# Post-norm stack with sparse experts: the loads of the experts' results issued in both arms of the branch, three unused products instead of five

## The chip, the cores and the metric

The kernel runs on one core of one Trainium2 chip. The metric is the device time of one execution in microseconds (us). The kernel before took 748.87 us, the median of three runs from 746.87 to 749.79.

## The reference

Two layers work on 2048 tokens of width 128. The change lies behind the last of their parts, a mixture of experts:

```python
probs = softmax(flat @ router_w)
topw, topi = top_k(probs, 2)                       # two of E = 8 experts for each token
combine = sum(one_hot(topi, E) * topw[..., None], axis=1)
h = silu(einsum('td,edf->tef', flat, w1) + b1)     # F = 512
y = einsum('tef,efd->ted', h, w2) + b2
out = einsum('te,ted->td', combine, y)
x = layernorm(x + (res + out))                     # then the last norm, and the output
```

Each token's output is the normed sum of a part that the kernel has in SBUF (`x4s`) and of the weighted results of the token's two experts.

## The kernel before

The tokens are 16 tiles of 128 in four blocks of four (`NB` = 4, `TB` = 4). Each token's row is first scattered to a DRAM table `xr`, sorted by expert, by indirect DMAs of GpSimd's queue. The experts then work on blocks of 256 rows (`BK`), each for one expert: `fetch_rows` (line 1379) loads a block from `xr` through SP's queue, `copy_weights` picks the expert's weights on VectorE, `first` and `second` (lines 1413 and 1426) are the two products with the activation between them, and `back` turns the result (line 1439), weighs it (line 1442) and scatters it by two indirect DMAs (line 1444) to a DRAM table `yr` of 4096 rows: row t holds token t's first expert's result, row 2048 + t its second's.

Since every expert's last block may be partly empty, up to 23 blocks (`NBK`) can be needed, and the number needed, `many`, is known at run time only. The first 19 blocks (`OFTEN`) always run. The last four stand under a branch, line 1490, which every engine takes for itself. The arm that is run when there are no more than 19 blocks holds no line of the source. The build puts steps into it that raise the completion counters (semaphores) by what the other arm would have raised, so that the counters agree behind the branch whichever arm ran. SP and ACT's transfers share eight such counters and take them in turn; GpSimd's indirect DMAs have another eight.

Behind the branch comes the last part. For each of the four blocks b, two loads of 256 KB bring the results of the first and second experts from `yr` into SBUF tiles `yk`, one issued by SP and one by ACT (line 1507): eight loads in all, called first to eighth here in the order b = 0 (SP, ACT), b = 1 (SP, ACT) and so on. A product with the identity puts `x4s` into a PSUM tile `z5` for each block (line 1499, from line 1510), then five products that nobody reads follow (`warm`, line 1513), and then, block after block, two more products with the identity add the block's two `yk` tiles (`sum_up`, line 1499 from line 1519). An fp32 product is two passes of TensorE. Of each block, VectorE then takes the statistics (lines 1043, 1044 and 1524), GpSimd the root (line 1066), VectorE the shift (line 1531), and ACT, with VectorE's help in the last block, writes the normed rows (lines 1048 and 1538), which SP stores (line 1541). This order is held on each engine as written.

Of the kernel before, what the change touches and what calls it, by code (L numbers as in the profile page):

```python
# [9 lines left out]
F32 = mybir.dt.float32  # L10
# [8 lines left out]
P = 128  # L19
# [8 lines left out]
def tile_postln_stack(ctx: ExitStack, tc: tile.TileContext, a: dict, out: bass.AP):  # L28
    nc = tc.nc
    T, D = a["x"].shape  # L30
    NT = T // P
    TB = 4
    BW = TB * P
    NB = NT // TB
# [9 lines left out]
    NBK = 2 * T // BK + E - 1  # L44
# [81 lines left out]
    def bc(v):  # L126
        return v.unsqueeze(1).to_broadcast([P, TB, D])
# [25 lines left out]
    with ExitStack() as l0:  # L153
# [419 lines left out]
        for k in range(NQ):  # L573
            b = k // 2
# [449 lines left out]
    for e in range(0, E, 2):  # L1024
        nc.sync.dma_start(
            out=wall[:, e : e + 2],
            in_=a["we"].rearrange("(e p) c -> p e c", p=P)[:, e : e + 2],
# [10 lines left out]
    lm = ctx.enter_context(tc.tile_pool(name="l1m", bufs=3))  # L1038
# [273 lines left out]
    for step in SEQUENCE.split():  # L1312
        name, of = step.split(":")
# [45 lines left out]
    def registers(n, engine, top):  # L1359
# [10 lines left out]
    many = nc.values_load(  # L1370
        used[0:1, :],
        min_val=0,
        max_val=NBK,
        skip_runtime_bounds_check_because="so many blocks at most",
    )

    def fetch_rows(j):
        xb = lm.tile([P, KT, ROW], F32, name="xb", bufs=SOON + 2)
        nc.sync.dma_start(
            out=xb, in_=xr[bass.ds(firsts[j], BK), :].rearrange("(t p) c -> p t c", p=P)  # L1380
        )
        xbs[j] = xb
# [3 lines left out]
    def copy_weights(j):  # L1386
        wt = lm.tile([P, WC], F32, name="wt", bufs=AHEAD)
        nc.vector.tensor_copy(wt, flat[:, bass.ds(offsets[j], WC)])
        wts[j] = wt

    def turn_rows(j):
        xb = xbs[j]
        pt = ps.tile([P, KT, P], F32, tag="p", name="px5")
        for t in range(KT):
            nc.tensor.transpose(pt[:, t, :], xb[:, t, 0:D], ident)  # L1395
        xT = lm.tile([P, BK], F32, name="xT5")
        nc.vector.tensor_scalar(
            xT,
            pt.rearrange("p t d -> p (t d)"),
            cols[:, 2:3],  # L1400
            cols[:, 3:4],
            ALU.mult,
            ALU.add,
        )
        xTs1[j] = xT

    def first(j):
        wt, xT = wts[j], xTs1.pop(j)
        hu = lm.tile([P, NF, BK], F32, name="hu", bufs=2)
        for f in range(0, NF, 2):  # L1410
            pu = ps_a.tile([P, 2, BK], F32, tag="acc", name="pu")
            for n in range(2):
                nc.tensor.matmul(pu[:, n], wt[:, ts(f + n, P)], xT, start=True, stop=True)  # L1413
                nc.scalar.activation(  # L1414
                    hu[:, f + n],
                    pu[:, n],
                    AF.Silu,
                    bias=wt[:, 2 * NF * P + f + n : 2 * NF * P + f + n + 1],
                )
        hus[j] = hu  # L1420

    def second(j):
        wt, hu = wts.pop(j), hus.pop(j)
        acc = ps_a.tile([P, BK], F32, tag="acc", name="acc")
        for f in range(NF):
            nc.tensor.matmul(  # L1426
                acc, wt[:, ts(NF + f, P)], hu[:, f], start=(f == 0), stop=(f == NF - 1)
            )
        yT = lm.tile([P, KT, P], F32, name="yT5")
        nc.vector.tensor_scalar(  # L1430
            yT.rearrange("p t d -> p (t d)"), acc, wt[:, WC - 1 : WC], None, ALU.add
        )
        yTs[j] = yT

    def back(j):
        xb, yT = xbs.pop(j), yTs.pop(j)
        pt = ps.tile([P, KT, P], F32, tag="p", name="py5")
        for t in range(KT):
            nc.tensor.transpose(pt[:, t, :], yT[:, t, :], ident)  # L1439
        yb = lm.tile([P, KT, D], F32, name="yb")  # L1440
        for t in range(KT):
            nc.vector.tensor_scalar_mul(yb[:, t], pt[:, t], xb[:, t, D + 1 : D + 2])  # L1442
        for t in range(KT):
            put = nc.gpsimd.indirect_dma_start(  # L1444
                out=yr[:, :],
                out_offset=bass.IndirectOffsetOnAxis(
                    ap=xb.bitcast(U32)[:, t, D : D + 1], axis=0
                ),
                in_=yb[:, t, :],
                in_offset=None,  # L1450
                bounds_check=2 * T - 1,
                oob_is_err=False,
            )
            tc.declare_no_dep(put.ins, group="back", reason="every row is written once")
            tc.add_to_no_dep_group("back", put.ins)
        return put

    def experts(begin, end):

        put = None  # L1460
        for j in range(begin, min(begin + AHEAD - 1, end)):
            copy_weights(j)
        for j in range(begin, min(begin + SOON, end)):
            fetch_rows(j)
        turn_rows(begin)
        for j in range(begin, end):
            if j + SOON < end:
                fetch_rows(j + SOON)
            first(j)
            if j + 1 < end:  # L1470
                turn_rows(j + 1)
            if j > begin:
                put = back(j - 1)
            second(j)
            if j + AHEAD - 1 < end:
                copy_weights(j + AHEAD - 1)
            if 4 <= j < 4 + NB:
                bt = ts(j - 4, TB)
                with tc.issue_after(put.ins):
                    nc.gpsimd.tensor_tensor(x3s[:, bt, :], x3s[:, bt, :], bc(mixc), ALU.subtract)  # L1480
            if 4 + NB <= j < 4 + 2 * NB:
                bt = ts(j - 4 - NB, TB)
                with tc.issue_after(put.ins):
                    nc.gpsimd.tensor_tensor(x4s[:, bt, :], x3s[:, bt, :], x4s[:, bt, :], ALU.add)
        back(end - 1)


    OFTEN = NBK - E // 2
    experts(0, OFTEN)
    with tc.If(many > OFTEN, preferred_fallthrough_block=False):  # L1490
        experts(OFTEN, NBK)

    y_v = yr.rearrange("(k n p) d -> k p n d", k=2, p=P)


    yks, zs, mvs, rs, nbs = {}, {}, {}, {}, {}

    def add(b, src, start, stop):
        nc.tensor.matmul(  # L1499
            zs[b], ident, src.rearrange("p t d -> p (t d)"), start=start, stop=stop  # L1500
        )

    for b in range(NB):
        bt = ts(b, TB)
        yk = [lm.tile([P, TB, D], F32, tag="mid", name=f"yk{k}", bufs=8) for k in range(2)]
        for k in range(2):
            (nc.sync, nc.scalar)[k].dma_start(out=yk[k], in_=y_v[k, :, bt, :])
        yks[b] = yk
        zs[b] = ps.tile([P, BW], F32, tag="p", name="z5")
        add(b, x4s[:, bt, :], True, False)  # L1510
    warm = ps_a.tile([P, BW], F32, tag="acc", name="warm2")
    for _ in range(5):
        nc.tensor.matmul(
            warm, ident, x4s[:, NT - TB :].rearrange("p t d -> p (t d)"), start=True, stop=True
        )
# [100 lines left out]
```

## Time and profile before

| | |
|---|---|
| median of three runs | 748.87 us |
| the profiled execution: its time | 749.07 us |
| its span, first to last instruction | 747.4 us |
| mean granted TensorE clock | 0.961 |
| PE, DVE, ACT, POOL busy | 89%, 72%, 63%, 26% |
| indirect DMAs of line 1444 | 38, two for each of 19 blocks: the arm with the last four blocks did not run |
| last of these begins on POOL | 721.61 us |
| loads of line 1507 begin | 725.84 us |
| first add of a `yk` begins on PE | 729.85 us |
| last work of VectorE on the output | 742.50 us |

Times in the trace are in microseconds from the span's start. PE is TensorE, PEld its weight loads, DVE is VectorE, POOL is GpSimd; a q behind an engine's name means its instruction queue, where branches, counter steps and DMA issues stand. Between the profiled execution's span and its time lie 1.67 us.

### The profile page before, as it was taken

To read this page: it belongs to the slowest core of one execution; us is meant where nothing else is said; L and a number is where in the kernel's file an instruction comes from. 1 tells how busy PE (TensorE), PEld (TensorE's weight loads), DVE (VectorE), ACT (ScalarE), POOL (GpSimd) and SP (SyncE) were. 2 spreads that over 40 slices of the span, in tenths; PEclk is the share of its full clock that TensorE was granted. 3 is DMA by queue.
4 is the path that set the end of the run, shared out by engine and by line. 5 is a ranking of instruction groups with operands and counts; after the bars stand their busy time and mean duration, and the time that the engine had idled before them with its cause. 6 is when DMAs were issued, how large, how long until landed. Compare 5 with 4: busy or idle time off the path is not lost. (4 is left out here: it accounts for less than half of the span.)

```text
span 747.4 us, 10679 instructions
## 1 busy us (share of the span) xinstructions
PE 662.8 (89%) x3745; PEld 376.5 (50%) x3745; DVE 535.4 (72%) x893; ACT 469.4 (63%) x1080; POOL 196.8 (26%) x203
## 2 busy tenths in 40 slices
PE   8989999999889988998799988799999805999984
PEld 7766655444346543533343333246567502688851
DVE  2566798897689887987899879796895634365524
ACT  1768798877787886877697778644455522344412
POOL 2311210112020130200500004014342676268632
PEclk9989999999999999999999999899999956999998
DMA  5902240210000205200069930150500011312115
GB/s 132 269 3 58 57 100 16 58 40 17 1 1 1 57 4 113 57 0 1 0 128 204 192 57 1 40 103 13 215 1 4 29 40 39 80 58 63 36 36 154
DMA packets 43622, 46.29 MB, mean 62 GB/s; under 512 B 3164, under 2 KB 33378, under 8 KB 43568
## 3 DMA queue, kind: packets, MB, share of 16 engines
q1 hardware_dynamic: 38896, 39.79, 23.8%
q0 software_dynamic: 2272, 4.24, 1.6%
q10 hardware_dynamic: 2400, 1.57, 0.8%
q8 instruction: 30, 0.49, 0.3%
q14 instruction: 24, 0.20, 0.1%
HBM read 23.13 MB, written 14.45 MB: 50 GB/s over the span
## 5 line engine op out<-in xcount | busy, mean ns | idle before, releaser
L637 ACT ACTIVATE sc<-sc,nmx 128x1024 f32<-128x1024 f32 (+7 forms) x384 | 321.6, 838 | 98.7 <-DVE nmx L634 65.4
L619 PE MATMUL sc<-kT,q 64*128 64x512 f32 (+7 forms) x1536 | 297.1, 509 | 19.0 <-ACT sc L637 17.9
L634 DVE TENSOR_REDUCE nmx<-sc 128x1 f32<-128x1024 f32 (+3 forms) x256 | 273.6, 1116 | 33.3 <-PE sc L619 19.8
L619 PEld LDWEIGHTS sc<-kT,q 64*128 64x128 f32 x1536 | 122.1, 187 | 143.1 <-ACT sc L637 86.7
L342 POOL TENSOR_TENSOR prod<-q,kT 128x1024 f32<-128x1024 f32 x16 | 37.4, 2348 | 203.5 <-PE pdl L354 68.9
L637 ACT ACTIVATION_READ_ACCUMULATOR sc<-sc,nmx 128x1 f32 x384 | 75.8, 197 | 0.0
L1414 ACT ACTIVATE hu<-pu,wt 128x256 f32<-128x256 f32 x76 | 33.4, 474 | 59.6 <-PE pu L1413 56.6
L627 DVE TENSOR_REDUCE nmx<-sc 128x2 f32<-128x256 f32 (+3 forms) x64 | 51.6, 818 | 11.7 <-PE sc L611 11.1
L94 POOL TENSOR_TENSOR ln_rs<-ln_rs,half_m 128x4 f32<-128x4 f32 x8 | 8.3, 1038 | 182.6 <-DVE ln_rs L93 182.6
L611 PE MATMUL sc<-rmask,lmask 64*128 64x64 bf16 x512 | 50.7, 190 | 0.0
L1444 POOL DMA_INDIRECT yr<-yb,xb x38 | 41.2, 1085 | 35.3 <-DVE yb L1442 28.4
L1413 PE MATMUL pu<-xT,wt 128*128 128x256 f32 x152 | 41.1, 393 | 0.1
L611 PEld LDWEIGHTS <-lmask 64*128 64x128 bf16 x512 | 28.0, 102 | 20.6 <-issue 13.4
L1276 POOL DMA_INDIRECT xr<-rows,slots x32 | 32.0, 999 | 19.9 <-issue 15.1
L1426 PE MATMUL acc<-hu,wt 128*128 128x256 f32 x152 | 35.9, 379 | 0.0
L317 PE MATMUL pq<-x2T,pq 128*128 128x256 f32 x128 | 33.5, 407 | 1.2 <-DMA pq<-in_pq_dram 0.6
L445 PE MATMUL pv<-x2T,pv 128*128 128x512 f32 x64 | 32.2, 633 | 2.6 <-DVE wx L451 2.2
L457 PE MATMUL py<-wx,po 128*128 128x512 f32 x64 | 30.8, 612 | 0.0
L1413 PEld LDWEIGHTS pu<-xT,wt 128*128 128x128 f32 x152 | 26.7, 189 | 7.6 <-ACT hu L1414 3.5
L317 PEld LDWEIGHTS pq<-x2T,pq 128*128 128x128 f32 x128 | 24.2, 198 | 11.0 <-ACT sc L637 6.3
L1426 PEld LDWEIGHTS acc<-hu,wt 128*128 128x128 f32 x152 | 27.5, 190 | 3.2
L1430 DVE TENSOR_SCALAR yT<-acc,wt 128x256 f32<-128x256 f32 x19 | 9.2, 484 | 23.4 <-PE acc L1426 23.3
(268 smaller groups left out, 798.5 us busy)
## 6 DMA issues: line engine op xcount, KB each, us to landing
xr<-pad SPq DMA_DIRECT2D x10, 845.0 KB
q<-q SPq DMA_DIRECT2D x32, 256.0 KB
wx<-wd SPq DMA_DIRECT2D x8, 1024.0 KB
wall<-in_we_dram SPq DMA_DIRECT2D x4, 1029.0 KB
xb<-xr SPq DMA_DIRECT2D x19, 130.0 KB
x2T<-in_xT_dram SPq DMA_DIRECT2D x4, 256.0 KB
xs<-in_x_dram SPq DMA_DIRECT2D x4, 256.0 KB
yk<-yr SPq DMA_DIRECT2D x4, 256.0 KB
```

The lines of the kernel that those rows point to most:

```text
L317: nc.tensor.matmul(pm[:, n // 2, ts(n % 2, QW)], pq[:, ts(c + n, P)], x2T[:, ts(k, QW)], start=True, stop=True,)
L342: nc.gpsimd.tensor_tensor(prod, q.rearrange("p c (t e r) -> p c t e r", e=2, r=HT)[:, :, :, eo], kT[:, :, eo, ts(k, QT), :], ALU.mult,)
L445: nc.tensor.matmul(pm[:, j], pv[:, ts(c + j, P)], x2T[:, ts(b, BW)], start=True, stop=True)
L611: nc.tensor.matmul(o[:, w - HT :], lmask[r, eo], rmask[r], start=False, stop=True,)
L619: nc.tensor.matmul(o, qs[k][eo][r, c, ts(t, P)], kT[r, c, eo, n0 : n0 + nt, :], start=True, stop=(g < NG - 1),)
L627: nc.vector.tensor_reduce(nm, sc.rearrange("p e (j x) -> p j e x", j=2)[:, :, :, :w], AX.XY, ALU.min,)
L634: nc.vector.tensor_reduce(nm, sc[:, :, :w], AX.XY, ALU.min)
L637: nc.scalar.activation(o, o, AF.Exp, bias=nm[:, n : n + 1], scale=-1.0, accum_out=sm[:, i % TB, 2 * c + j, g : g + 1],)
L1413: nc.tensor.matmul(pu[:, n], wt[:, ts(f + n, P)], xT, start=True, stop=True)
L1414: nc.scalar.activation(hu[:, f + n], pu[:, n], AF.Silu, bias=wt[:, 2 * NF * P + f + n : 2 * NF * P + f + n + 1],)
L1426: nc.tensor.matmul(acc, wt[:, ts(NF + f, P)], hu[:, f], start=(f == 0), stop=(f == NF - 1))
L1444: put = nc.gpsimd.indirect_dma_start(out=yr[:, :], out_offset=bass.IndirectOffsetOnAxis(ap=xb.bitcast(U32)[:, t, D : D + 1], axis=0), in_= ...
```

## The change

The eight `yk` tiles are allocated ahead of the branch. A function `load_results` issues the eight loads, in the same order and from the same two queues. It is called at the end of the arm with the last four blocks, and it is the whole of a written `Else` arm. Behind the branch the loads are gone, and of the five unused products three are left.

```diff
     OFTEN = NBK - E // 2
     experts(0, OFTEN)
-    with tc.If(many > OFTEN, preferred_fallthrough_block=False):
+
+    y_v = yr.rearrange("(k n p) d -> k p n d", k=2, p=P)
+    yks = {
+        b: [lm.tile([P, TB, D], F32, tag="mid", name=f"yk{k}", bufs=8) for k in range(2)]
+        for b in range(NB)
+    }
+
+    def load_results():
+        for b in range(NB):
+            for k in range(2):
+                (nc.sync, nc.scalar)[k].dma_start(out=yks[b][k], in_=y_v[k, :, ts(b, TB), :])
+
+    with tc.If(many > OFTEN, preferred_fallthrough_block=False) as more:
         experts(OFTEN, NBK)
-
-    y_v = yr.rearrange("(k n p) d -> k p n d", k=2, p=P)
-
-
-    yks, zs, mvs, rs, nbs = {}, {}, {}, {}, {}
+        load_results()
+    with more.Else():
+        load_results()
+
+    zs, mvs, rs, nbs = {}, {}, {}, {}
...
     for b in range(NB):
         bt = ts(b, TB)
-        yk = [lm.tile([P, TB, D], F32, tag="mid", name=f"yk{k}", bufs=8) for k in range(2)]
-        for k in range(2):
-            (nc.sync, nc.scalar)[k].dma_start(out=yk[k], in_=y_v[k, :, bt, :])
-        yks[b] = yk
         zs[b] = ps.tile([P, BW], F32, tag="p", name="z5")
         add(b, x4s[:, bt, :], True, False)
     warm = ps_a.tile([P, BW], F32, tag="acc", name="warm2")
-    for _ in range(5):
+    for _ in range(3):
         nc.tensor.matmul(
```

## The prediction

> **What bounds the kernel now.** I read the page for the share of each engine, then followed only the last 30 us, since nothing ahead of the branch is touched. PE is 89% busy over the span, but the page's share says nothing of this tail: there the chain of waits runs through two transfers.
>
> ```profile
> 721.19 0.42 POOLq L1370
> 721.61 4.21 DMA yr<-yb,xb
> 725.82 0.02 issue
> 725.84 3.97 DMA yk<-yr
> 729.81 0.04 issue
> 729.85 5.84 PE z L1499 x12
> ...
> 735.71 0.31 DVE ln_st L1043
> ```
>
> The last scatter of the experts' results begins at 721.61, the loads of these results begin at 725.84, and the adds begin at 729.85. The 4.21 us are not all transfer. Asked for DMA packets from 723.5 to 726, the trace has none. What fills that stretch is shown by the instructions of the branch's own line:
>
> ```profile
> L1490 SPq EVENT_SEMAPHORE  x4: 17/17/17, 694.9 to 695.1; - x4
> L1490 POOLq EVENT_SEMAPHORE  x4: 17/43/43, 721.8 to 724.2; - x4
> ...
> L1490 POOLq COMPARE_BRANCH  x2: 37/38/40, 721.7 to 725.9; - x2
> ...
> L1490 POOLq INC_SWDGE_SEM  x1: 1616/1616/1616, 724.3 to 724.3; - x1
> ```
>
> These are the steps of the arm that holds no source. GpSimd waits for its scatters until 724.2, then raises their eight counters in an instruction of 1.616 us, and SP and ACT start the loads only when it is through. SP's four steps make up for the four row fetches of the other arm; they ran at 695, long before.
>
> ```profile
> 724.74 4.46 PE L1513 MATMUL warm<-x4s,ident 128*128 128x512 f32 x10
> 729.85 7.57 PE L1499 MATMUL z<-yk,ident 128*128 128x512 f32 x16 [0.66 <-DMA yk<-yr]
> ```
>
> In PE's timeline the five unused products (ten passes, 0.43 us apart) end at 729.20, 0.66 us before the first load is there. The weight loads show which later adds wait for their load, the fifth, the sixth and the seventh:
>
> ```profile
> 733.43 0.30 PEld L1499 LDWEIGHTS z<-yk,ident 128*128 128x128 f32 x2 [0.70 <-DMA yk<-yr]
> 734.55 0.30 PEld L1499 LDWEIGHTS z<-yk,ident 128*128 128x128 f32 x2 [0.82 <-DMA yk<-yr]
> 735.44 0.30 PEld L1499 LDWEIGHTS z<-yk,ident 128*128 128x128 f32 x2 [0.59 <-DMA yk<-yr]
> ```
>
> From the first statistics on, VectorE sets the pace: they start at 731.87, 733.70, 735.71 and 737.61 for the four blocks, 1.83 to 2.01 us apart. So what moves block 0's statistics moves the end, one for one.
>
> **Part 1, the loads leave GpSimd's step.** Inside the arm a load waits for the last scatter itself. The row fetches at the start of the expert part do the same with the scatters of `xr`. The load then begins when GpSimd's waits end, 1.616 us plus a wait of 43 ns and small gaps before 725.84: 1.75 us earlier, at 724.09. Bounds: 1.6 us (the instruction alone) to 2.3 us (the last packets end by 723.5). SP and ACT reach the arm long before (695, 718). Transfers and issue order stay, so all eight landings move by 1.75 us.
>
> **Part 2, what the adds wait for.** The loads now stand in two arms, and the adds behind both. An add must wait for its load as either arm issues it. The eight counters of SP's and ACT's transfers are dealt out in turn, and each arm starts at the same place of the ring. In the arm with four more blocks, four fetches take four counters first, so the n-th load there has the counter that in the other arm belongs to load n + 4. In the arm that runs, the adds of loads 1 to 4 then wait for loads 5 to 8 as well. For loads 5 to 8 the second wait is on a counter which SP makes up, as it does now in four steps of 17 ns, when load 4 is there; that is no later. No row shows this wait; it is read from how the program is dealt out, and its bounds are nothing (the counters agree) and a wait for all eight loads.
>
> Its price: the first add needs the fifth load, 733.43 - 1.75 = 731.68. The second needs the sixth, 734.55 - 1.75 = 732.80. Block 0's statistics now start 1.05 us after the third of its four passes (730.82 to 731.87) and after a wait PE's next pass comes 0.1 us later, so they would start at 733.96. That is 2.1 us later than 731.87, the gain of part 1 already taken off. The third add needs the seventh load, 733.69, and block 1 is ready at 735.8, just when VectorE is (733.96 + 1.83). The later blocks find everything there. The 2.1 us pass to the end. Queued behind the waiting add are only the other adds. ACT's next work waits 18.3 us for PE today, SP's next store starts at 737.34, so what these two do in the arm has cover of more than 5 us.
>
> **Part 3, two products fewer.** Four passes of 0.43 us, 1.72 us: PE ends its unused work at 727.48. If the first load were enough (728.06 by part 1), that is just in time, and five products would have been 1.1 us too late. With part 2, PE idles from 727.48 to 731.68, 4.2 us. What such a gap does is seen elsewhere in the trace, stage by stage with the granted clock (third from the right):
>
> ```profile
> 290.28:293.69 3.41, 1.24 (x8) 0.67 (x7) 2.01 (x2) 0.00 (x0) 0.00 (x0) 1.00 0.03 5
> 293.69:297.10 3.41, 3.41 (x7) 0.95 (x7) 3.41 (x4) 3.03 (x6) 0.00 (x0) 0.50 0.00 0
> 297.10:300.51 3.41, 3.41 (x18) 1.93 (x16) 3.07 (x5) 2.25 (x6) 0.00 (x0) 1.00 0.02 5
> ```
>
> A gap of 2.17 us (290.79 to 292.96) is followed by 3.41 us at a clock of 0.50, and only then is it 1.00 again. At 0.50 a pass takes 0.85 us. Block 0's first two passes would end at 733.4, 0.6 us after the sixth load, and the other two cost 0.5 us more: 1.1 us. If the slow stretch lies early, nothing but block 0 is hit; if late, it misses block 0 but holds block 1; if it lasts two stretches, both (6.83 us at 0.50 followed the gap of 5.13 us before 480.42). Bounds 0 and 2.1 us; I take 1.1, which is nearest to the single stretch.
>
> The Trainium skill, page "TensorE: Matmul & The Clock Gate", section "Why this matters for your kernels", asks for no idle gap of PE above about 3 us. By it, leaving five products would have kept the gap at 2.5 us and the clock up, so these two products alone would be worth the 1.1 us; by the row above, where 2.17 us were enough, they need not be.
>
> **Costs taken as nothing.** The other arm's eight more issues: it is not run (38 scatters are 19 blocks). Longer arms in the instruction stream: hidden by SP's wait of 30.4 us and ACT's of 7 us before the loads, 0 to 0.5 us if that cover went. Allocating the tiles earlier moves no instruction.
>
> **Sum.** On the profiled execution's 749.07 us (span 747.4 and 1.67 outside): -1.75 (part 1), +3.85 (part 2 against it, net 2.1), +1.1 (clock) = +3.2, or 752.3. It lies 0.2 above the median of the runs, 748.87, so I say 752.1. With the bounds of the clock, 751.0 to 753.1.
>
> **The rivals.** *Straight gain* (ends on the other side): the adds wait for their own loads only. Then part 1 is all there is; PE is free at 727.48, the first load is there at 728.06, the gap is 0.6 us and leaves the clock alone, and block 0's statistics start at 730.1. 748.87 - 1.75 = 747.1. For it: the chain above names nothing between the loads and VectorE's pace but the loads. Against it: two arms with different numbers of transfers on one ring of counters. It decides as soon as the counter that the first add waits for is raised by the first load alone, before 731.87 - 2.02 = 729.85.
> *Same counters, late make-up*: the loads of both arms get the same counters, and the makeup falls on loads 5 to 8. SP then raises these counters only when the eighth load is there, about 733.8 + 0.2; block 2 is ready at 734.0 + 0.1 + 3 x 0.43 + 0.63 = 736.0 and not 735.71. Net +0.3: 749.2. Against it: both arms start at one place of the ring.
> *Wait for everything*: the first add waits for all eight loads, to about 734.0, block 0's statistics start at 736.0, 4.1 later, and the clock takes 1.1 to 1.5: 748.87 + 5.4 = 754.3. Against it: today's loads wait behind the branch for the last scatter's counter, not for every one of the branch.
>
> **How the numbers follow.** Crossed waits 0.66, straight gain 0.20, late make-up 0.07, wait for everything 0.07. 0.5%, 3.7 us, is about what a measurement of this kernel can tell from no change. Crossed waits, 2.1 to 4.2 us slower, and with runs that scatter by 2.9 us, fall on either side of it; I give half, 0.33, and all of the last rival: slower 0.40. The straight gain passes it only with scatter, a quarter: faster 0.05. Within: 0.55. The range reaches from the straight gain with some scatter, 746.5, to the crossed waits' upper bound with some, 754.0. The forecast's own range is 751.0 to 753.1.
>
> **What would show it.** Loads at 724.1 and INC_SWDGE_SEM beside them, not ahead: part 1. PE's first add near 731.7 and waits for `yk` ahead of the first, second and third add, though the first load landed near 728: part 2. A clock of 0.50 over 730 to 734: part 3. Loads still at 725.8 would make part 1 wrong. A first add at 728.1 would make the forecast wrong and the straight gain right.

## The result, and the profile after

The changed kernel takes 750.18 us and the kernel before 748.62 us, medians of 22 runs each. The ratio is 1.0028, with a 95% interval of 1.0015 to 1.0041: slower by about 2.1 us (the two medians lie 1.6 us apart). In the profiled execution the last scatter begins at 720.24 us, where it began at 721.61 before; from there to the span's end it is 28.4 us, before 25.8. So the tail, as this stretch is called below, is 2.6 us longer in that execution, and the stages ahead, which nothing changed, happened to end 1.4 us earlier. All times below that are counted "from the last scatter's start" leave this out.

In the chain of waits the adds now follow a later load:

```profile
724.37 7.66 DMA yk<-yr
732.03 0.04 issue
732.07 1.14 PE z L1513 x2
733.21 0.02 issue
733.24 0.31 DVE ln_st L1043
```

The load of the chain was issued at 724.37, the third of ACT's four, which is the sixth of all. It holds up PE's second add at 732.07, although this add sums the second load. The weight loads show a wait for loads ahead of the first add as well:

```profile
730.51 0.30 PEld L1513 LDWEIGHTS z<-yk,ident 128*128 128x128 f32 x2 [0.90 <-DMA yk<-yr]
732.07 0.30 PEld L1513 LDWEIGHTS z<-yk,ident 128*128 128x128 f32 x2 [1.26 <-DMA yk<-yr]
```

The first add begins 7.5 us after the first load was issued at 723.01; in the kernel before that load took 3.97 us. The next view lists the instructions of the branch's line, now 1502, and at its end who waited for them:

```profile
L1502 POOLq EVENT_SEMAPHORE  x4: 17/43/43, 720.5 to 723.1; - x4
...
L1502 POOLq INC_SWDGE_SEM  x1: 1616/1616/1616, 723.2 to 723.2; - x1
L1502 ACTq EVENT_SEMAPHORE  x1: 17/17/17, 725.8 to 725.8; - x1
...
  PE warm L1523: 2.3, 1
```

GpSimd's step of 1.616 us is still there, from 723.2, but the loads no longer wait for it: they begin at 723.01. New is what the last line shows: PE's unused products waited 2.3 us for ACT's counter step, which ran at 725.8. PE's timeline shows both:

```profile
719.89 3.67 PE L1513 MATMUL z<-x4s,ident 128*128 128x512 f32 x8 [1.59 <-PEq L1502]
725.91 4.54 PE L1523 MATMUL warm<-x4s,ident 128*128 128x512 f32 x6 [2.35 <-ACTq L1502]
730.52 1.13 PE L1513 MATMUL z<-yk,ident 128*128 128x512 f32 x2
732.07 6.28 PE L1513 MATMUL z<-yk,ident 128*128 128x512 f32 x14 [0.43 <-DMA yk<-yr]
```

Six passes of unused products take 4.54 us where ten took 4.46 before. The busy times by stretch say why: the granted clock, third from the right, is 0.50 after the gap.

```profile
722.68:726.09 3.41, 1.06 (x4) 0.24 (x3) 0.00 (x0) 0.00 (x0) 0.00 (x0) 1.00 0.42 109
726.09:729.50 3.41, 3.41 (x5) 1.35 (x5) 0.00 (x0) 0.00 (x0) 0.00 (x0) 0.50 1.20 311
729.50:732.91 3.41, 2.91 (x7) 0.90 (x6) 0.00 (x0) 0.00 (x0) 0.00 (x0) 1.00 0.82 197
```

The slow stretch lies under the unused products, and the clock is back at 1.00 when the first add begins.

### The profile page after: what moved, and what is told of

It is laid out like the page before. It is cut to its first block, busy times and chain, and to the rows that moved or that the text cites. A ratio compares the mean times of both kernels' runs of the same rounds, so it can differ in the third digit from the quotient of the medians.

```text
span 748.6 us, 10675 instructions
## 1 busy us (share of the span) xinstructions
PE 662.6 (89%) x3741; PEld 376.4 (50%) x3741; DVE 534.8 (71%) x893; ACT 469.0 (63%) x1080; POOL 196.6 (26%) x203
## 5 line engine op out<-in xcount | busy, mean ns | idle before, releaser
L627 DVE TENSOR_REDUCE nmx<-sc 128x2 f32<-128x256 f32 (+3 forms) x64 | 51.5, 817 | 11.7 <-PE sc L611 11.1
L1444 POOL DMA_INDIRECT yr<-yb,xb x38 | 41.2, 1084 | 35.3 <-DVE yb L1442 28.4
L317 PE MATMUL pq<-x2T,pq 128*128 128x256 f32 x128 | 31.8, 391 | 1.0 <-DMA x2T<-in_xT_dram 0.5
L1426 PEld LDWEIGHTS acc<-hu,wt 128*128 128x128 f32 x152 | 27.5, 190 | 3.2
```

The costliest lines, as they stand in the source:

```text
L317: nc.tensor.matmul(pm[:, n // 2, ts(n % 2, QW)], pq[:, ts(c + n, P)], x2T[:, ts(k, QW)], start=True, stop=True,)
L627: nc.vector.tensor_reduce(nm, sc.rearrange("p e (j x) -> p j e x", j=2)[:, :, :, :w], AX.XY, ALU.min,)
L1426: nc.tensor.matmul(acc, wt[:, ts(NF + f, P)], hu[:, f], start=(f == 0), stop=(f == NF - 1))
L1444: put = nc.gpsimd.indirect_dma_start(out=yr[:, :], out_offset=bass.IndirectOffsetOnAxis(ap=xb.bitcast(U32)[:, t, D : D + 1], axis=0), in_= ...
```

## The experiments

The theory after the result has three parts: the adds wait on crossed counters; the unused products wait for ACT's counter step; a gap of PE halves the clock, and what that costs depends on which products it falls on. The rivals are named with each run. Every kernel is timed against the kernel before. The table counts in microseconds from the last scatter's start in the profiled execution.

| kernel | loads begin | first add | block 0's statistics | span's end | ratio (95% interval) |
|---|---|---|---|---|---|
| before | 4.2 | 8.2 | 10.3 | 25.8 | 1 |
| changed | 2.8 | 10.3 | 13.0 | 28.4 | 1.0028 (1.0015 to 1.0041) |
| e1_same_counters | 2.7 | 9.8 | 11.7 | 27.0 | 1.001 (0.9995 to 1.0024) |
| e2_same_counters_z | 2.8 | 6.8 | 8.8 | 24.5 | 0.9961 (0.9944 to 0.9978) |
| e3_crossed_z | 2.8 | 10.2 | 14.0 | 30.4 | 1.005 (1.0034 to 1.0066) |
| e4_before_three | 4.5 | 8.5 | 11.5 | 27.5 | 1.0004 (0.9989 to 1.0019) |
| e5_two_ahead_z | 2.7 | 8.5 | 11.5 | 27.5 | one run |
| e6_six_ahead_z | 2.8 | 12.6 | 16.4 | 31.7 | one run |
| e7_no_branch | 2.3 | 6.5 | 8.4 | 23.8 | 0.9981 (0.9962 to 1.0000) |
| e8_same_counters_none | 2.8 | 6.8 | 10.7 | 26.8 | 1.0025 (1.001 to 1.004) |

**The same counters in both arms, e1_same_counters.** Four spare transfers in the arm that is not run move its loads on by four places of the ring of eight counters, so that each load has the same counter in both arms.

```diff
         experts(OFTEN, NBK)
+        for n in range(4):
+            spare = lm.tile([P, len(COLS)], F32, name="spare", bufs=4)
+            nc.sync.dma_start(out=spare, in_=a["cols"])
         load_results()
```

> The changed kernel with four spare small transfers on SP's queue ahead of the loads in the arm that is not run. Each load then has the same completion counter in both arms, and no add waits for a load that is not its own. Theory (two waits: the adds on crossed counters, and the unused products on a step that ACT takes in its arm behind its four load issues): the unused products still begin about 5.7 us after the last scatter's start and hold PE to about 10.2, so the first add begins there (10.3 in the changed kernel) and block 0's statistics at about 12.2 instead of 13.0; time 1 to 2 us over the kernel before. Rival (the crossed counters are the whole loss): first add at about 6.9 after the last scatter's start, statistics at 8.8, time 1.5 us under the kernel before.

PE's timeline:

```profile
726.51 4.47 PE L1526 MATMUL warm<-x4s,ident 128*128 128x512 f32 x6 [2.14 <-ACTq L1502]
730.81 7.03 PE L1516 MATMUL z<-yk,ident 128*128 128x512 f32 x16
```

The 16 passes of the adds now run without a wait for any load, so the crossed waits are gone. But they begin only when the unused products are through, 9.8 from the last scatter's start. Statistics came at 11.7, 0.5 earlier than expected, and the time is 0.7 us over the kernel before (0.4 under to 1.8 over), where 1 to 2 were expected. The rival, with 6.9 and 8.8, is out: the crossed counters are not the whole loss.

**Free of ACT's step as well, e2_same_counters_z.** The unused products go into the last block's own sum, whose tile does not wait for anything that ACT does in its arm.

```diff
+        if b == NB - 1:
+            for _ in range(3):
+                add(b, x4s[:, bt, :], True, True)
         add(b, x4s[:, bt, :], True, False)
-    warm = ps_a.tile([P, BW], F32, tag="acc", name="warm2")
-    for _ in range(3):
...
```

> As the one with the same counters, and the three unused products go into the last block's sum ahead of its own product, so that they wait for nothing that ACT does. Theory: unused products right behind the others, to about 7 us after the last scatter's start; first add at 6.8 to 7.0, block 0's statistics at 8.8, against 10.3 in the kernel before; time 1.5 us under the kernel before (747.1 on a median of 748.6). Rival (the issue inside the arm brings nothing, the transfers get slower by what they start earlier): statistics at 10 or later, time within 0.5 us of the kernel before.

```profile
721.08 6.25 PE L1516 MATMUL z<-x4s,ident 128*128 128x512 f32 x14 [1.56 <-PEq L1502]
728.26 4.56 PE L1516 MATMUL z<-yk,ident 128*128 128x512 f32 x10 [0.94 <-DMA yk<-yr]
733.16 2.84 PE L1516 MATMUL z<-yk,ident 128*128 128x512 f32 x6 [0.34 <-DMA yk<-yr]
```

First add at 6.8, statistics at 8.8, both as expected to 0.1. This version beats both kernels: 745.97 us, ratio 0.9961. The runs gain 2.9 us (1.7 to 4.2), the profiled tail 1.3; the expected 1.5 lies just below the interval. The profiled execution, 747.68 us, is the third longest of the twelve. Where the rest comes from stays open.

**Crossed counters without the wait for ACT, e3_crossed_z.** The same edit of the unused products on the changed kernel, no spare transfers. Here the gap stands where the prediction put it, behind the unused products.

> The changed kernel, crossed counters and all, with the three unused products in the last block's sum, free of ACT's step. Theory: the unused products end about 6.7 us after the last scatter's start, PE then idles until the fifth load at 10.2, and this gap halves the clock under block 0's adds: statistics at 13.0 without the clock, 13.5 to 14.2 with it; time 2.6 to 3.8 us over the kernel before, up to 1.2 over the changed kernel. Rival (the unused products' late start is what costs the time): first add at 8 or earlier, time at or under the kernel before.

PE's timeline, the load that the chain of waits names ahead of the first add (SP's third, the fifth of all), and the stretches around this add:

```profile
719.69 6.25 PE L1513 MATMUL z<-x4s,ident 128*128 128x512 f32 x14 [1.59 <-PEq L1502]
730.22 10.09 PE L1513 MATMUL z<-yk,ident 128*128 128x512 f32 x16 [4.29 <-DMA yk<-yr]
```

```profile
723.83 6.34 DMA yk<-yr
```

```profile
729.30:732.72 3.42, 2.50 (x3) 1.13 (x4) 0.00 (x0) 0.00 (x0) 0.00 (x0) 0.51 0.81 194
732.72:736.10 3.38, 3.38 (x5) 1.35 (x4) 1.75 (x9) 0.00 (x0) 0.06 (x1) 0.50 0.00 0
736.10:739.50 3.40, 3.40 (x9) 1.52 (x8) 2.39 (x13) 0.51 (x2) 1.58 (x2) 0.99 0.00 0
```

PE waits 4.29 us for the fifth load, and two stretches at half clock fall on the adds: 10.09 us for the 16 passes. Slower than before by 0.5%, 3.7 us, within the 2.6 to 3.8 expected. The rival falls: with the unused products on time the first add comes no earlier (10.2 against 10.3), and the profiled tail is 2.0 us longer than the changed kernel's, whose late unused products had covered the gap. Over the runs, the intervals of the two ratios overlap.

**Three products alone, e4_before_three.** `range(5)` becomes `range(3)` in the kernel before.

> The kernel before with three unused products instead of five, nothing else. Both theories: PE idles about 2.4 us before the first add. If that is enough to halve the clock, block 0's statistics move by up to 1.1 us and the time by 0 to 1.1; if not, no difference.

```profile
723.99 2.74 PE L1513 MATMUL warm<-x4s,ident 128*128 128x512 f32 x6
729.37 8.83 PE L1499 MATMUL z<-yk,ident 128*128 128x512 f32 x16 [2.64 <-DMA yk<-yr]
```

In the profiled execution the gap of 2.64 us does halve the clock (8.83 us for the adds against 7.57) and the tail grows by 1.7 us, 0.2 of it because the loads begin that much later; over 12 runs the ratio is 1.0004, at most 1.4 us over the kernel before. The profiled execution, 750.05 us, is the second longest of the twelve. The mean granted clock was 0.955 to 0.958 in ten of the twelve runs, and 0.959 or 0.961 in 21 of the 29 of the kernel before; one stretch of 3.41 us at half the clock takes 0.002 off the mean. So the slow stretch may well come in most executions, but a run's mean clock does not say where its slow stretches lie, and why the runs lose less than the profile shows stays open.

**The dose, e5_two_ahead_z and e6_six_ahead_z.** e2_same_counters_z with six and with two spare transfers instead of four: the first add is then held by the third and by the seventh load.

> As the one with the same counters and the unused products in the last block's sum, but with six spare transfers in the arm that is not run: the counters of the first two loads are then those of the third and the fourth in the arm that runs. Theory: PE's first add begins when the third load is there (about 8.3 after the last scatter's start), its second when the fourth is (about 9.3), block 0's statistics at about 10.5, against 8.8 with the same counters and 10.3 in the kernel before. Rival (the crossed counters matter only by the clock): first add at 6.8.

> The same with two spare transfers: the first two adds then wait for the seventh and the eighth load as well. Theory: first add at about 12.0 after the last scatter's start, second not before 12.6, and after a gap of 5.3 us at half the clock: block 0's statistics at 15.4 to 16 (14.0 with the fifth and the sixth load, e3_crossed_z). Rival: first add no later than e3_crossed_z's 10.2.

```profile
730.07 8.84 PE L1516 MATMUL z<-yk,ident 128*128 128x512 f32 x16 [2.65 <-DMA yk<-yr]
```

```profile
733.30 8.98 PE L1516 MATMUL z<-yk,ident 128*128 128x512 f32 x16 [6.62 <-DMA yk<-yr]
```

The first line is of e5, the second of e6. The chains of waits name the loads ahead of these adds, SP's second and SP's fourth:

```profile
724.78 5.15 DMA yk<-yr
```

```profile
725.13 8.12 DMA yk<-yr
```

The first add follows the counters: 6.8 (e2_same_counters_z), 8.5 (e5), 10.2 (e3_crossed_z) and 12.6 (e6) from the last scatter's start as it is held by the first, third, fifth and seventh load. Of what runs, e5 differs from e2_same_counters_z only in the counts that the steps add; e6 also has two steps of 0.017 us fewer. Expected were 8.3 and about 12.0; neither rival came true. The statistics of e5 came 1.0 later than expected, since its gap of 2.65 us halved the clock, which the expectation had left out; those of e6 came 0.4 beyond its range.

**Without the branch, e7_no_branch.**

```diff
-    with tc.If(many > OFTEN, preferred_fallthrough_block=False) as more:
-        experts(OFTEN, NBK)
-        load_results()
-    with more.Else():
-        load_results()
+    load_results()
...
```

Not shown are the six unused products in the last block's sum, twice the number of e2_same_counters_z, and the loading of `many`, which goes with the branch.

> The branch and the last four blocks are left out (they are not run with these inputs); the loads follow the first 19 blocks directly, with six unused products in the last block's sum, since PE comes to them 1.6 us earlier. It shows what the branch costs beyond the crossed counters. Theory: the loads begin 2.8 after the last scatter's start, the first add at 6.8, block 0's statistics at 8.8, as with the same counters, so the time is that of e2_same_counters_z within 1 us. Rival (the branch and its steps still cost time there): 1.5 us or more below it.

```profile
718.85 8.75 PE L1503 MATMUL z<-x4s,ident 128*128 128x512 f32 x20
727.44 7.52 PE L1503 MATMUL z<-yk,ident 128*128 128x512 f32 x16
```

Loads, first add and statistics come 0.3 to 0.5 earlier than expected. The tail is 0.7 us shorter than that of e2_same_counters_z, and the runs are not faster than its runs: the intervals overlap. So e2_same_counters_z has got back nearly all that the branch cost here.

**No unused products, e8_same_counters_none.** e2_same_counters_z with `range(0)`.

> The same counters in both arms, no unused products at all. PE idles from about 3.5 to 6.8 after the last scatter's start. Theory: the gap of 3.3 us halves the clock for 3.4 us or more, block 0's statistics come at 9.9 to 10.6 instead of 8.8, block 1 waits too in some executions: 1 to 2.5 us over e2_same_counters_z. Rival (the unused products do nothing once the loads come earlier): the same time as e2_same_counters_z.

```profile
726.86 9.82 PE L1516 MATMUL z<-yk,ident 128*128 128x512 f32 x16 [3.55 <-DMA yk<-yr]
```

The gap of 3.55 us makes the adds 9.82 us long. Statistics came at 10.7, just beyond the 9.9 to 10.6 expected. The tail is 2.3 us over that of e2_same_counters_z, as expected, the runs 0.64%, 4.8 us, which is more than expected. With the same counters the whole gain hangs on the three unused products.

## Why the prediction was right, and where it was not

Forecast was 3.2 us slower, with 2.1 to 4.2 as its own range; measured are 2.1 (1.1 to 3.1), just at the lower end; as a time, 750.18 us lies below the 751.0 to 753.1 given. The direction came from the right step, the size partly from a wrong one. In the profiled tail two misses partly cancel: parts 1 and 2 together cost 2.7 us instead of 2.1, and the 1.1 us of part 3 are missing.

- *Part 1*, the loads leave GpSimd's step: right. They begin 1.46 us earlier from the last scatter's start (2.77 against 4.23), not 1.75. GpSimd's last wait also ended later, 2.9 us after the scatter's start (720.24 to 723.1) against 2.6, so that much was the scatter's own landing.
- *Part 2*, the crossed counters: right, and shown by the dose. From the last scatter's start, the first add was due at 10.07 and came at 10.28; the second was due at 11.19 and came at 11.83. ACT's four issues took 2.78 us, from 723.02, where they took 2.15: a counter step stands between the first two (723.8), and the fourth took 0.87 us, where none took more than 0.52 before; the reason of that is open. Statistics 2.7 us later than before, where 2.1 were forecast.
- *Part 3* failed at "PE ends its unused work at 727.48". I let the unused products follow the others at once. Their tile had to wait for ACT's counter step, which stands behind ACT's loads in the arm; "what these two do in the arm has cover of more than 5 us" was wrong of ACT, because I looked only at ACT's next work and not at who waits for its counter. The gap came ahead of the unused products, the slow clock fell on them, and the 1.1 us for it were nothing. That it cost nothing was luck: the unused products ended at 730.45, just ahead of the first add at 730.52, and in e1_same_counters the same late start held the adds. e3_crossed_z shows the term as it was meant: 1.0 us on block 0's statistics (14.0 against 13.0) and, with two slow stretches, 2.0 us at the span's end, which is near the upper bound of 2.1. One row was read too simply: the slow stretch of 6.83 us did not only follow the gap of 5.13 us, it began at 478.01, inside the gap.
- *The rivals*. The straight gain needed two things that the change did not have, the same counters and unused products free of ACT; with both, e2_same_counters_z takes it. The late make-up did not occur: SP's and ACT's steps on these counters stand ahead of the loads or among the first of them, the last at 723.8. The wait for everything did not occur either: the second add was let go by the sixth load.
- *The page's rule*. In the changed kernel a gap of PE of 2.35 us was followed by 3.41 us at a clock of 0.50. The Trainium skill, page "TensorE: Matmul & The Clock Gate", section "Why this matters for your kernels", asks for no gap above about 3 us; in this case a shorter one was enough.

## What to carry to other kernels

When work moves into the arms of a branch, look at the counters that the arms share: if the arms issue different numbers of transfers, a reader behind them can wait for later transfers than its own, as the adds did here, and a few transfers in the arm that is rarely run can put this right. Look also at every step that an engine does in an arm for the sake of the counters: it stands behind what the engine issues there, and who waits for it is not seen in that engine's own next work. Products that keep a clock up must be tied to nothing that the change makes late.

## What was not expected of the hardware

A late start of unused products can be worth something: the half clock after a gap of PE fell on them in the changed kernel, and when they came in time (e3_crossed_z) it fell on the adds and the profiled tail was another 2.0 us longer. GpSimd's counter step took 1.616 us for eight counters in every profile of a kernel with the branch, while SP's and ACT's steps took 0.017 us each.
